# A transformer block with cross-attention and MLP on one core: batches 2 to 4 of the MLP loaded and normalised sooner, the steps between attention and MLP in another order

## The chip, the cores and the metric

The kernel runs on one core of a Trainium2 chip. The metric is device time in microseconds (us). A core has TensorE (PE: matmuls and transposes), VectorE (DVE), ScalarE (ACT), GpSimd (POOL) and SyncE (SP, which here issues the DMAs). Each engine works through its own queue in order, and waits by semaphores for results of the others and for transfers.

## The reference

One block of a diffusion transformer, with x and the context 16 x 256 x 256, a condition vector for each of 16 batches, 16 heads of 16 and an MLP of width 1024, all in fp32:

```python
c_proj = silu(c) @ W_mod + b_mod
shift_a, scale_a, gate_a, shift_m, scale_m, gate_m = split(c_proj, 6)
q, k, v = heads(modulate(_ln(x), shift_a, scale_a) @ W_qkv + b_qkv)
x = x + gate_a[:, None] * (softmax(q @ k.T * scale) @ v @ W_proj + b_proj)
q_c = heads(_ln(x) @ W_qc + b_qc)
k_c, v_c = heads(_ln(context) @ W_kvc + b_kvc)
x = x + (softmax(q_c @ k_c.T * scale) @ v_c @ W_cproj + b_cproj)
h = gelu(modulate(_ln(x), shift_m, scale_m) @ W_mlp1 + b_mlp1) @ W_mlp2 + b_mlp2
x = x + gate_m[:, None] * h
```

## The kernel before

**Units and beats.** The attention is cut into 32 units, one for each batch and kind: self-attention (names with `_s`, then the batch) and cross-attention (`_c`), the last units being c10 (unit 26) to c15 (unit 31). A unit is 8 beats. In a beat `beat(n, k)` TensorE computes scores of the next unit (`s`, to find the row maxima `mx`) and of this one (`st`), while pieces of the neighbours are laid between: the projections of unit n+2, the transposes of n+3, the layernorm of n+4, the load of n+5, the output projection of n-1. The table `PLAN` names these pieces by short words, beat by beat. fp32 products are made of a high and a low part (`xTh`, `xTl`; `wkch`, `wkcl`), so each is three matmuls; POOL makes most of the splits (a CAST for the high part, a subtraction for the low one).

**Order.** All instructions go through `InOrder` (line 51 in the profile), which keeps each engine's program order as written. So an instruction that waits holds up everything behind it on its engine. Only ScalarE is left to the compiler's scheduler from chunk 23 of the MLP on (`'AP': 23`).

**The MLP.** After unit 31 comes the tail: 16 batches of 4 chunks, numbered 0 to 63. With chunk i TensorE runs the first matmul (`ph_b_c`, 12 matmuls) of chunk i+2 and the second (`s` or `st` from `hh`, `hl`; 12 matmuls) of chunk i-1; ScalarE makes gelu twice (`hf` in fp32, `hh` rounded), POOL the rest `hl`. First matmuls of batches 0 and 1 run before that, in units 30 and 31 (`ps_h`, parked in `hk` and `v`); ph_1_3 is the last of them. Before a batch's first matmul its rows must be loaded back from DRAM (`mlp_load`, tile `x2_b`; the store is `x2d`), given the projection's bias (`mlp_bias`, POOL, x + cb), measured (`mlp_stats`, DVE, `st_m`, `mv_m`, with a reciprocal root `rs_m` on POOL) and normalised (`mlp_apply`, DVE, `xn_m`). Batch 2 is transposed by TensorE (`mlp_T(2)`). From batch 3 on `mlp_apply` transposes blocks on DVE (`blk_m`) and sends them by four DMAs to `turned`; `mlp_fetch` brings them back by four DMAs (`raw_m`), and `mlp_T` scales them on ScalarE (`xTf_m`) and splits them on POOL into `wkch`, `wkcl` (even batches) or `wqch`, `wqcl` (odd ones), which ph reads.

**Where batches 0 to 4 are prepared.** Batches 0 and 1 take the places of units 32 and 33 in the beats: load by the word `ld` at beat 1 and bias by `c2` at beat 2 of the unit four ahead of them. The steps of batch 2 hang on numbers in `E_['M']` = (7, 9, 13, 15), for load, bias, statistics and apply: number p means unit 31 + p // 16, beat (p % 16) // 2, here beats 3, 4, 6 and 7 of unit 31. Batch 3 is loaded after the last beat; its bias comes with chunk 0, its statistics with chunk 1, its `mlp_apply` with chunk 3, its fetch with chunk 4. Between the last beat and chunk 0 stand the last attention pieces: `av_part` (TensorE's `o`), `q.proj` (output projection of c14, `psP_c14`), then `o.turn(1)` and `o.norm(1)` (copy `oT_31_3`, transposes `psA1_c15`, normalised `A_c15`).

**The late query layernorm.** For the first and the last two cross units the layernorm of the query (`st_q`, `rs_q`, `xn_q`) is made one unit later than for the others, by ScalarE (words L1, L2, L3, with a factor `nb_q` on DVE); for the rest it is made on POOL (words e5, e6).

Of the kernel before, what the change touches and what calls it, by code (L numbers as in the profile page):

```python
# [21 lines left out]
def pixart_block(  # L22
# [8 lines left out]
    B, N, H = x.shape  # L31
# [76 lines left out]
    brow = const.tile([32, P], F32, name="brow")  # L108
# [147 lines left out]
    wm = []  # L256
# [9 lines left out]
    gm = []  # L266
# [850 lines left out]
    def beat(n, k):  # L1117
# [133 lines left out]
    for i, (b, c) in enumerate(chunks):  # L1251
        ACT.on = i < E_['AP']
        if 2 < i < len(chunks) - 1:
            mlp_gelu(*chunks[i + 1])
        if i in turns:
            mlp_T(turns[i])
        if c == 3 and b + 3 in BY_DVE:
            mlp_apply(b + 3)
        if c == 0 and b + 2 in BY_DVE:
            mlp_fetch(b + 2)  # L1260
        if i in firsts:
            mlp_first(*chunks[firsts[i]])
        if i > 0:
            mlp_second(*chunks[i - 1])
        for f in pst.get(i, ()):
            f()
        ahead = b + 2 if 2 < b + 2 < B else None
        soon = ahead if ahead and ahead in BY_DVE else None
        if c == 0 and ahead and not soon:
            mlp_bias(ahead)  # L1270
        if c == 0 and b + 3 in BY_DVE:
            mlp_bias(b + 3)
        if c == 1:
            if b + 1 < B:
                mlp_gates(b + 1)
            if b + 3 in BY_DVE:
                mlp_stats(b + 3)
                M[b + 3].ln.pow()
            if ahead and not soon:
                mlp_stats(ahead)  # L1280
        if c == 2 and ahead and not soon:
            M[ahead].ln.pow()
        if c == 2 and 4 <= b + 4 < B:
            mlp_load(b + 4)
        if c == 3:
            if ahead and not soon:
                mlp_apply(ahead)
            mlp_residual(b)
# [49 lines left out]
```

## Time and profile before

| | us |
|---|---|
| runs | 742.74, 743.11, 747.35 |
| median | 743.11 |
| the profiled execution | 747.66 |
| its span | 745.9 |
| outside the span | 1.76 |

The profile shows one execution, which is 4.55 us above the median of the runs. Times in a row are its start and its duration, counted from the start of the span; a name has its buffer number left out, so `xn_m` stands for every batch. A bracket behind a row is the idle time of the engine ahead of it and what ended that. All rows have line 51, since the helper records every operation.

### The profile page before, as it was taken

How to read it: one execution, taken by the hardware profiler on the slowest of the kernel's cores; microseconds unless marked ns; L12 is line 12 of the kernel's file. 1: busy time of each engine (PE TensorE's matmuls, PEld its weight loads, DVE VectorE, ACT ScalarE, POOL GpSimd, SP SyncE). 2: the span in 40 equal slices, each digit the busy share in tenths (PEclk: the TensorE clock that was granted, in tenths of full speed). 3: DMA queues.
4: the chain of work that ended last, by engine and by line, in shares of the span. 5: the costliest groups of instructions: out<-in, count | busy, mean ns of one | idle time of the engine just before them, and what ended most of it. 6: DMA issues, size and time to landing. Idle time of an engine off the chain costs nothing.

```text
span 745.9 us, 25386 instructions
## 1 busy us (share of the span) xinstructions
PE 731.3 (98%) x10092; PEld 644.4 (86%) x10092; DVE 569.1 (76%) x1165; ACT 563.6 (76%) x978; POOL 520.2 (70%) x636
## 2 busy tenths in 40 slices
PE   9999999999999999999999999999999998999997
PEld 8778888888888888888888888878879998999997
DVE  4888888988888888888889889898727664546542
ACT  4278888888888888888888888888895665666663
POOL 6756676857667485665758678667566887788872
PEclk9999999999999999999999999999999999999999
DMA  6755445443544545354544545544122544443430
GB/s 207 199 147 154 133 127 143 121 131 102 171 118 127 145 117 146 107 165 131 143 135 121 163 127 162 155 122 122 59 73 58 156 132 104 109 127 97 114 81 34
DMA packets 108906, 94.81 MB, mean 127 GB/s; under 512 B 36914, under 2 KB 92756, under 8 KB 108788
## 3 DMA queue, kind: packets, MB, share of 16 engines
q1 hardware_dynamic: 108308, 92.27, 44.5%
q8 instruction: 80, 1.31, 0.7%
q0 software_dynamic: 192, 0.52, 0.3%
q10 hardware_dynamic: 288, 0.39, 0.2%
q14 instruction: 38, 0.31, 0.1%
HBM read 30.38 MB, written 11.86 MB: 57 GB/s over the span
## 4 chain that ended last, share of the span: by engine, by line
PE 92%; DVE 2%; ACT 1%; POOL 1%; issue 1%; DMA 1%; SPq 1%; ACTq 0%; DVEq 0%; POOLq 0%
PE s L51 17%; PE st L51 16%; PE o L51 16%; PE ph L51 9%; PE ps_q L51 5%; PE ps_qc L51 4%; PE ps_kc L51 3%; PE ps_P_s L51 3%; PE ps_v_c L51 3%; PE ps_k L51 3%; PE ps_v_s L51 2%; PE ps_P_c L51 2%; PE ps_h L51 1%; PE psT_q L51 1%; PE psA_c L51 1%
## 5 line engine op out<-in xcount | busy, mean ns | idle before, releaser
L51 DVE TENSOR_REDUCE mx<-s 128x2 f32<-128x512 f32 x504 | 324.3, 682 | 63.3 <-PE s L51 56.8
L51 ACT ACTIVATE pt<-st 128x1024 f32<-128x1024 f32 x252 | 259.0, 1028 | 17.5 <-PE st L51 11.7
L51 PE MATMUL s<-big 63*128 63x256 f32 (+1 forms) x1024 | 184.1, 298 | 0.6 <-DVE mx L51 0.4
L51 PEld LDWEIGHTS s<-big 63*128 63x128 f32 (+1 forms) x1024 | 133.6, 185 | 19.8 <-DVE l_kc L51 6.6
L51 PE MATMUL st<-big 64*128 64x256 f32 (+1 forms) x1024 | 133.8, 298 | 0.3 <-ACT pt L51 0.2
L51 PE MATMUL o<-pt,v 128*32 128x256 f32 x2048 | 123.8, 382 | 0.0
L51 PEld LDWEIGHTS st<-big 64*128 64x128 f32 (+1 forms) x1024 | 95.5, 185 | 16.3 <-issue 12.9
L51 POOL TENSOR_TENSOR hl<-hf,hh 128x512 fp32r<-128x512 f32 x64 | 86.5, 1359 | 28.0 <-ACT hh L51 28.0
L51 PEld LDWEIGHTS o<-pt,v 128*32 128x32 f32 x2048 | 60.0, 109 | 41.5
L51 ACT ACTIVATE hh<-ph,bT 128x256 fp32r<-128x256 f32 x114 | 48.0, 474 | 24.3 <-PE st L51 12.4
L51 ACT ACTIVATE hf<-ph,bT 128x256 f32<-128x256 f32 x114 | 47.7, 472 | 22.5 <-PE ph L51 22.5
L51 ACT COPY oT<-o 128x512 f32<-128x512 f32 x63 | 36.9, 586 | 32.6 <-PE o L51 32.6
L51 PE MATMUL st<-big,hh 128*128 128x256 f32 x256 | 47.6, 285 | 0.0
L51 PE MATMUL ph<-wkch,wself 128*128 128x256 f32 x224 | 44.8, 284 | 2.4 <-ACT hh L51 2.4
L51 DVE TENSOR_SCALAR xn_m<-x,mv_m,rs_m 128x256 f32<-128x256 f32 x28 | 31.5, 1165 | 20.3 <-POOL rs_m L51 20.3
L51 PE MATMUL s<-big,hh 128*128 128x256 f32 x256 | 46.8, 282 | 0.0
L51 PE MATMUL ph<-wqch,wself 128*128 128x256 f32 x224 | 44.6, 282 | 1.3 <-ACT hh L51 1.3
L51 PE MATMUL ps_k<-xTh_s,wself 64*128 64x256 f32 (+1 forms) x232 | 43.9, 294 | 0.0
L51 PE MATMUL ps_q<-xTh_s,wself 64*128 64x256 f32 (+1 forms) x240 | 39.7, 283 | 0.4 <-DVE l_q L51 0.4
L51 PEld LDWEIGHTS st<-big,hh 128*128 128x128 f32 x256 | 39.9, 193 | 0.0
L51 POOL CAST xTh_c<-y_c 128x512 fp32r<-128x512 f32 x16 | 9.8, 612 | 43.1 <-ACT y_c L51 43.1
L51 PE MATMUL ps_v_s<-wself,xTh_s 64*128 64x256 f32 x224 | 39.2, 294 | 0.0
(249 smaller groups left out, 2500.1 us busy)
## 6 DMA issues: line engine op xcount, KB each, us to landing
big<-h_kc SPq DMA_DIRECT2D x64, 128.0 KB
big<-h_qc SPq DMA_DIRECT2D x64, 128.0 KB
big<-h_k SPq DMA_DIRECT2D x62, 128.0 KB
big<-h_q SPq DMA_DIRECT2D x62, 128.0 KB
big<-l_k SPq DMA_DIRECT2D x32, 128.0 KB
big<-l_q SPq DMA_DIRECT2D x32, 128.0 KB
g<-gd SPq DMA_DIRECT2D x16, 256.0 KB
c<-in_ctx_dram SPq DMA_DIRECT2D x16, 256.0 KB
```

The lines of the kernel that those rows point to most:

```text
L51: i = f(*a, **k)
```

## The change

In six places the order is written anew; the matmuls stay the same.

- The four steps of batch 2 (`E_['M']`) move from unit 31 to unit 30, beats 3 and 6 (load, bias), and to unit 31, beats 0 and 2 (statistics, apply).
- Batch 3 is loaded at beat 4 of unit 31, its bias made ahead of the first gelu, its statistics right after `o.norm(1)`, its `mlp_apply` with chunk 1, its fetch with chunk 2. Batch 4 is loaded after the last beat.
- `q.proj(0)` and `q.proj(1)` come ahead of `av_part(last, 2)` and `(last, 3)`, and `mlp_first` of chunk 7 (ph_1_3) behind them and the first gelu. So TensorE runs psP_c14, o, ph_1_3 instead of ph_1_3, o, psP_c14.
- c14 is no longer late: its query layernorm is made in unit 26 on POOL instead of in unit 27 on ScalarE.
- Batches 0 and 1 are loaded by the word `lc` at beat 5 of the unit before, and their bias is made at beat 1 (`c1`) instead of beat 2.
- Loads of batches 5 and up are issued ahead of the batch's gate load (`gm`) instead of behind it.

```diff
...
                 return tc.keep_in_program_order(i) if self.on else i
             return issue
 
-    E_ = {'M': (7, 9, 13, 15),
...
+    E_ = {'M': (-10, -4, 1, 5),
...
 
     PE = InOrder(nc.tensor, True)
     ACT, DVE, POOL, SP = (InOrder(e, True) for e in (nc.scalar, nc.vector, nc.gpsimd, nc.sync))
...
     def end(p, f, *a):
         at_end[p // 16 - 1, p % 16].append(lambda: f(*a))
 
+    end(8, mlp_load, 3)
     for p, f in zip(E_['M'], (mlp_load, mlp_bias, lambda b: mlp_stats(b, True), mlp_apply)):
         end(p, f, 2)
 
...
         lc = q4 if q4 and q4.kind == "c" else None
         ls = q4 if q4 and q4.kind in ("s", "m") and q4.ln else None
         lx = q3 if q3 and q3.kind == "c" else None
-        late = lx and lx.b in (0, B - 2, B - 1)
-        early = lc if lc and lc.b not in (0, B - 2, B - 1) else None
-        c5 = unit(n + 5)
+        late = lx and lx.b in (0, B - 1)
+        early = lc if lc and lc.b not in (0, B - 1) else None
+        c5 = later_unit(n + 5)
         ln = lambda v, i: lambda *a: v.ln[i].steps
 
         def attention(v, hf):
...
             "pe": on(p2, lambda: p2.end()), "hadd": on(p2 and (p2.n == nu - 3), lambda: (p2.add(), p2.store())),
             "add": on(p3, lambda: p3.add()), "gate": on(p1, lambda: p1.gate()),
             "store": on(p3, lambda: p3.store()), "begin": lambda: cur.post.begin(),
-            "ld": on(ls and n > 0, lambda: load(ls)),
-            "lc": on(c5 and c5.kind == "c", lambda: load(c5)),
-            "c1": on(lc, lambda: lc.ln[0].steps[0]()),
-            "c2": on(lc or ls and ls.kind == "m", lambda: [f() for f in lc.ln[0].steps[1:]] if lc else mlp_bias(ls.b)),
+            "ld": on(ls and n > 0 and ls.kind == "s", lambda: load(ls)),
+            "lc": on(c5 and c5.kind != "s" and (c5.kind == "c" or c5.ln), lambda: load(c5)),
+            "c1": on(lc or ls and ls.kind == "m", lambda: lc.ln[0].steps[0]() if lc else mlp_bias(ls.b)),
+            "c2": on(lc, lambda: [f() for f in lc.ln[0].steps[1:]]),
             "s1": on(ls, lambda: ls.ln[0].steps[0]()),
             "s6": on(ls, lambda: ls.ln[0].steps[1]()),
             "s7": on(ls, lambda: ls.ln[0].steps[2]()),
...
     M[0].h[3] = tail[2].K.ps.rearrange("p (j n) -> p j n", j=2)
     for b in range(2):
         M[b].xT = M[b].src.xT
-    mlp_load(3)
+    mlp_load(4)
     mlp_gates(0)
     first_at = 7
-    mlp_first(*chunks[first_at])
+    q.proj(0)
+    q.proj(1)
     av_part(last, 2)
     av_part(last, 3)
+    mlp_bias(3)
     mlp_gelu(*chunks[0])
-    q.proj(0)
-    q.proj(1)
+    mlp_first(*chunks[first_at])
     mlp_gelu(*chunks[1])
     mlp_gelu(*chunks[2])
     mlp_gelu(*chunks[3])
     q.finish()
     o.turn(1)
     o.norm(1)
-    pst = {1: (lambda: mlp_T(2), o.aT.turn, o.aT.high, o.aT.low_dve), 4: (lambda: o.proj(0), lambda: o.proj(1), o.finish)}
+    mlp_stats(3)
+    M[3].ln.pow()
+    pst = {1: (lambda: mlp_T(2), o.aT.turn, o.aT.high, o.aT.low_dve, lambda: mlp_apply(3)),
+           2: (lambda: mlp_fetch(3),), 4: (lambda: o.proj(0), lambda: o.proj(1), o.finish)}
     turns = {}
     turns.update((NCH * b, b + 1) for b in range(2, B - 1))
     firsts = {5: 8}
...
             mlp_gelu(*chunks[i + 1])
         if i in turns:
             mlp_T(turns[i])
-        if c == 3 and b + 3 in BY_DVE:
+        if c == 3 and b > 0 and b + 3 in BY_DVE:
             mlp_apply(b + 3)
-        if c == 0 and b + 2 in BY_DVE:
+        if c == 0 and b > 1 and b + 2 in BY_DVE:
             mlp_fetch(b + 2)
         if i in firsts:
             mlp_first(*chunks[firsts[i]])
...
         soon = ahead if ahead and ahead in BY_DVE else None
         if c == 0 and ahead and not soon:
             mlp_bias(ahead)
-        if c == 0 and b + 3 in BY_DVE:
+        if c == 0 and b > 0 and b + 3 in BY_DVE:
             mlp_bias(b + 3)
         if c == 1:
             if b + 1 < B:
                 mlp_gates(b + 1)
-            if b + 3 in BY_DVE:
+            if b > 0 and b + 3 in BY_DVE:
                 mlp_stats(b + 3)
                 M[b + 3].ln.pow()
             if ahead and not soon:
                 mlp_stats(ahead)
         if c == 2 and ahead and not soon:
             M[ahead].ln.pow()
-        if c == 2 and 4 <= b + 4 < B:
+        if c == 0 and 4 < b + 4 < B:
             mlp_load(b + 4)
         if c == 3:
             if ahead and not soon:
```

VectorE at the end of unit 31, from the second half of c14's normalisation (`rc1`, `A_c14`) to the projection's gate (`t1_c14`), before:

```order
L51 RECIPROCAL rc1_c14_12183<-psA1_c14_12135 128x16
L51 TENSOR_TENSOR A_c14_12053<-psA1_c14_12135,rc1_c14_12183 128x4x64
L51 BN_STATS st_m2_12285<-x2_2_12186 128x6 x2
L51 BN_AGGR mv_m2_12288<-st_m2_12285 128x2 x2
L51 RECIPROCAL rc0_c15_12315<-psA0_c15_12260 128x16
L51 TENSOR_TENSOR A_c15_12314<-psA0_c15_12260,rc0_c15_12315 128x4x64
L51 TENSOR_SCALAR xn_m2_12318<-x2_2_12186,mv_m2_12288,rs_m2_12291 128x256 x2
L51 COPY oT_31_3_12355<-o_31_2_12338 128x512
L51 TENSOR_TENSOR t1_c14_12396<-psP_c14_12363,xg_14_9475 128x512
```

After, from the statistics of batch 2:

```order
L51 BN_STATS st_m2_12098<-x2_2_11894 128x6 x2
L51 BN_AGGR mv_m2_12101<-st_m2_12098 128x2 x2
L51 TENSOR_SCALAR xn_m2_12172<-x2_2_11894,mv_m2_12101,rs_m2_12104 128x256 x2
L51 RECIPROCAL rc1_c14_12198<-psA1_c14_12147 128x16
L51 TENSOR_TENSOR A_c14_12056<-psA1_c14_12147,rc1_c14_12198 128x4x64
L51 RECIPROCAL rc0_c15_12320<-psA0_c15_12274 128x16
L51 TENSOR_TENSOR A_c15_12319<-psA0_c15_12274,rc0_c15_12320 128x4x64
L51 COPY oT_31_3_12357<-o_31_2_12340 128x512
L51 TENSOR_TENSOR t1_c14_12399<-psP_c14_12327,xg_14_9475 128x512
```

The statistics and `xn_m2` moved from between c14 and the copy `oT_31_3` to ahead of c14's second half; the copy follows `A_c15` directly.

VectorE from there on to `xn_m3`, before:

```order
L51 TENSOR_TENSOR A_c15_12314<-psA1_c15_12399,rc1_c15_12404 128x4x64
L51 TENSOR_SCALAR xTf_m2_12425<-psT_m2_12420,sc1_103,cpT_101 128x256 x2
L51 TENSOR_TENSOR wkcl_96<-xTf_m2_12425,wkch_95 128x512
L51 TENSOR_TENSOR xTl_ac15_12437<-psT_ac15_12431,xTh_ac15_12436 128x512
L51 BN_STATS st_m3_12442<-x2_3_12321 128x6 x2
L51 BN_AGGR mv_m3_12445<-st_m3_12442 128x2 x2
L51 TENSOR_SCALAR xn_m3_12471<-x2_3_12321,mv_m3_12445,rs_m3_12448 128x8x32 x2
```

After:

```order
L51 TENSOR_TENSOR A_c15_12319<-psA1_c15_12402,rc1_c15_12407 128x4x64
L51 BN_STATS st_m3_12410<-x2_3_12229 128x6 x2
L51 BN_AGGR mv_m3_12413<-st_m3_12410 128x2 x2
L51 TENSOR_SCALAR xTf_m2_12436<-psT_m2_12431,sc1_103,cpT_101 128x256 x2
L51 TENSOR_TENSOR wkcl_96<-xTf_m2_12436,wkch_95 128x512
L51 TENSOR_TENSOR xTl_ac15_12448<-psT_ac15_12442,xTh_ac15_12447 128x512
L51 TENSOR_SCALAR xn_m3_12451<-x2_3_12229,mv_m3_12413,rs_m3_12416 128x8x32 x2
```

The statistics of batch 3 (`st_m3`, `mv_m3`) moved from behind `xTl_ac15` to ahead of `xTf_m2`.

POOL between the bias of batch 2 and that of batch 3, the last ahead of the MLP's `hl`, before (`big2` holds the second weight, `y_ac14` is c14's transposed output):

```order
L51 TENSOR_TENSOR x2_2_12186<-x2_2_12186,cb_106 128x512
L51 CAST xTh_ac14_12250<-y_ac14_12248 128x512
L51 TENSOR_TENSOR xTl_ac14_12251<-y_ac14_12248,xTh_ac14_12250 128x512
L51 TENSOR_TENSOR big2_77<-w2_7_11676,big2_77 128x512
L51 TENSOR_SCALAR rs_m2_12291<-mv_m2_12288 128x2
L51 TENSOR_TENSOR rs_m2_12291<-rs_m2_12291,mhalf_73 128x2
L51 TENSOR_TENSOR hl_0_0_12359<-hf_0_0_12357,hh_0_0_12358 128x512
L51 TENSOR_TENSOR hl_0_1_12378<-hf_0_1_12376,hh_0_1_12377 128x512
L51 TENSOR_TENSOR hl_0_2_12384<-hf_0_2_12382,hh_0_2_12383 128x512
L51 TENSOR_TENSOR hl_0_3_12390<-hf_0_3_12388,hh_0_3_12389 128x512
L51 TENSOR_TENSOR x2_3_12321<-x2_3_12321,cb_106 128x512
```

After, from `rs_m2` on, batch 2's bias being further ahead, behind c13's split:

```order
L51 TENSOR_SCALAR rs_m2_12104<-mv_m2_12101 128x2
L51 TENSOR_TENSOR rs_m2_12104<-rs_m2_12104,mhalf_73 128x2
L51 TENSOR_TENSOR big2_77<-w2_4_11725,big2_77 128x512
L51 TENSOR_TENSOR t1_c13_12145<-t1_c13_12145,xg_13_8712 128x512
L51 TENSOR_TENSOR big2_77<-w2_5_11154,big2_77 128x512
L51 CAST xTh_ac14_12264<-y_ac14_12262 128x512
L51 TENSOR_TENSOR xTl_ac14_12265<-y_ac14_12262,xTh_ac14_12264 128x512
L51 TENSOR_TENSOR big2_77<-w2_7_11676,big2_77 128x512
L51 TENSOR_TENSOR x2_3_12229<-x2_3_12229,cb_106 128x512
L51 TENSOR_TENSOR hl_0_0_12362<-hf_0_0_12360,hh_0_0_12361 128x512
```

The bias of batch 2 and `rs_m2` moved ahead of the last weight splits and c14's split; the bias of batch 3 moved from behind `hl_0_3` to ahead of `hl_0_0`.

More of the change, by code (lines that the diff above doesn't have):

```diff
@@ L53, in __getattr__ @@
             return issue
-    E_ = {'M': (7, 9, 13, 15), 'CUT': 8, 'LN': {'s': 'pool', 'c': 'pool', 'q': 'pool'}, 'ON': (1, 1, 1), 'L0': -16, 'L1': 1, 'S0': -7, 'A0': 0, 'T0': 1, 'S1': 5, 'A1': 7, 'L2': 9, 'T1': 9, 'S2': 32, 'AP': 23, 'DV': (0, 1), 'HP': (1, 0), 'BZ': {}, 'AV': {1: [(1, 2), (1, 3)], 9: [(0, 0), (0, 1)]}, 'AHEAD': (0, 0, 0, 0, 0, 2), 'TW': {(21, 6): 'cb', (23, 6): 'u1', (25, 1): 'u0', (25, 7): 'u2', (27, 1): 'u3', (27, 4): 'h2p', (27, 5): 'h3p', (28, 0): 'l2d', (28, 3): 'u5 h1p', (28, 4): 'h0p', (29, 0): 'l3', (29, 1): 'l0', (29, 3): 'l1d', (29, 6): 'u7', (29, 7): 'u4 u6 h4p', (30, 1): 'h5p h6d', (30, 7): 'l6', (31, 0): 'h7p', (31, 1): 'l4', (31, 2): 'l5', (31, 6): 'l7'}, 'XP': 1, 'IL': 1, 'MF': 0, 'SH': 4, 'RAMP': 1, 'HA': 1, 'MP': 16, 'W': (7, 1, 0, 0), 'PRE': 'z0qp z0kp load rest ld2 one0 silu b12 brow L0a turn L0b b4 L0d scale T0t sc1 hik lok L1a T0h L1b T0l b4 shift hiq K0a L1d bk loq K0m K0h K0x0 K0x1 K0y0p K0y1p T1t K0l T1h K0l0 K0l1 bq T1l Q0a Q0m Q0h Q0x0 Q0y0p Q0x1 Q0y1p Q0l Q0l0 Q0l1 z1kp z1qp K1a K1b hiv lov Q1a Q1b K1x0 K1x1 K1y0 K1y1 K1l K1l0 K1l1 Q1x0 Q1x1 Q1y0 Q1y1 Q1l Q1l0 Q1l1 L2a L2b L2c V0a V0b bv b9 ld3', 'SL': {(-1, 0): 'V1a', (-1, 1): 'T2t T2h T2p vone z2kp z2qp', (-1, 2): 'V1b', (-1, 3): 'rest wm', (-1, 4): 'M0 rest one1 ld4', (-1, 5): 'K2a L3a', (-1, 6): 'K2m L3b L3p L3c', (-1, 7): 'mods sc2 one2 rest', (0, 0): 'gm rest', (0, 1): 'rest', (0, 4): 'rest', (0, 6): 'rest', (1, 0): 'rest', (1, 5): 'rest'}}
@@ new lines, in pixart_block @@
+    E_ = {'M': (-10, -4, 1, 5), 'CUT': 8, 'LN': {'s': 'pool', 'c': 'pool', 'q': 'pool'}, 'ON': (1, 1, 1), 'L0': -16, 'L1': 1, 'S0': -7, 'A0': 0, 'T0': 1, 'S1': 5, 'A1': 7, 'L2': 9, 'T1': 9, 'S2': 32, 'AP': 23, 'DV': (0, 1), 'HP': (1, 0), 'BZ': {}, 'AV': {1: [(1, 2), (1, 3)], 9: [(0, 0), (0, 1)]}, 'AHEAD': (0, 0, 0, 0, 0, 2), 'TW': {(21, 6): 'cb', (23, 6): 'u1', (25, 1): 'u0', (25, 7): 'u2', (27, 1): 'u3', (27, 4): 'h2p', (27, 5): 'h3p', (28, 0): 'l2d', (28, 3): 'u5 h1p', (28, 4): 'h0p', (29, 0): 'l3', (29, 1): 'l0', (29, 3): 'l1d', (29, 6): 'u7', (29, 7): 'u4 u6 h4p', (30, 1): 'h5p h6d', (30, 7): 'l6', (31, 0): 'h7p', (31, 1): 'l4', (31, 2): 'l5', (31, 6): 'l7'}, 'XP': 1, 'IL': 1, 'MF': 0, 'SH': 4, 'RAMP': 1, 'HA': 1, 'MP': 16, 'W': (7, 1, 0, 0), 'PRE': 'z0qp z0kp load rest ld2 one0 silu b12 brow L0a turn L0b b4 L0d scale T0t sc1 hik lok L1a T0h L1b T0l b4 shift hiq K0a L1d bk loq K0m K0h K0x0 K0x1 K0y0p K0y1p T1t K0l T1h K0l0 K0l1 bq T1l Q0a Q0m Q0h Q0x0 Q0y0p Q0x1 Q0y1p Q0l Q0l0 Q0l1 z1kp z1qp K1a K1b hiv lov Q1a Q1b K1x0 K1x1 K1y0 K1y1 K1l K1l0 K1l1 Q1x0 Q1x1 Q1y0 Q1y1 Q1l Q1l0 Q1l1 L2a L2b L2c V0a V0b bv b9 ld3', 'SL': {(-1, 0): 'V1a', (-1, 1): 'T2t T2h T2p vone z2kp z2qp', (-1, 2): 'V1b', (-1, 3): 'rest wm', (-1, 4): 'M0 rest one1 ld4', (-1, 5): 'K2a L3a', (-1, 6): 'K2m L3b L3p L3c', (-1, 7): 'mods sc2 one2 rest', (0, 0): 'gm rest', (0, 1): 'rest', (0, 4): 'rest', (0, 6): 'rest', (1, 0): 'rest', (1, 5): 'rest'}}
```

## The prediction

> **What bounds the kernel now.** I read the page first, then busy time by stretch, then TensorE's timeline for its gaps, the chain that ended last, and the other engines' timelines at each gap. The page:
>
> ```profile
> PE 731.3 (98%) x10092; PEld 644.4 (86%) x10092; DVE 569.1 (76%) x1165; ACT 563.6 (76%) x978; POOL 520.2 (70%) x636
> ```
>
> TensorE is busy for 731.3 of 745.9 us. The change issues the same matmuls, so only the 14.6 us of gaps, and the clock, can move. By stretch (PE busy first, granted clock after POOL):
>
> ```profile
> core 0: us, PE busy (x) PEld busy (x) DVE busy (x) ACT busy (x) POOL busy (x), PEclk, DMA share, GB/s
> 100.00:490.00 390.00, 389.85 (x6403) 331.28 (x6404) 340.61 (x735) 330.46 (x512) 271.89 (x372) 1.00 0.48 135
> 490.00:580.00 90.00, 86.89 (x1194) 74.64 (x1187) 63.59 (x120) 69.00 (x118) 60.11 (x66) 1.00 0.32 90
> 580.00:620.00 40.00, 38.72 (x326) 38.35 (x325) 26.06 (x42) 26.76 (x64) 35.56 (x32) 1.00 0.51 136
> 620.00:660.00 40.00, 37.65 (x306) 37.44 (x305) 19.88 (x34) 22.79 (x55) 31.29 (x30) 0.96 0.41 109
> ```
>
> From 100 to 490 us the gaps come to 0.15 us: nothing is to be won there, only lost. The change works between 465 and 590 us. TensorE's own rows, the gap and its releaser in brackets, show what there is to win:
>
> ```profile
> 501.93 0.27 PE L51 MATMUL psm<-ident,mx 64*128 64x64 f32 x1 [0.84 <-ACT oT L51]
> 560.15 0.66 PE L51 MATMUL psA_c<-ident,oT 128*128 128x128 f32 x4 [1.06 <-DVE oT L51]
> 578.11 0.39 PE L51 MATMUL st<-big,hl 128*128 128x256 f32 x1 [0.56 <-POOL hl L51]
> 583.22 0.35 PE L51 MATMUL ph<-wqch,wself 128*128 128x256 f32 x1 [0.83 <-ACT hh L51]
> 584.03 0.38 PE L51 MATMUL ph<-wqcl,wself 128*128 128x256 f32 x1 [0.45 <-POOL wqcl L51]
> 626.20 0.38 PE L51 MATMUL ph<-wkch,wself 128*128 128x256 f32 x1 [2.35 <-ACT hh L51]
> ```
>
> The first five, 0.84 + 1.06 + 0.56 + 0.83 + 0.45 = 3.74 us, lie where the change works and are the most that it can win in its own place. The sixth is far behind it, and is dearer than its 2.35 us. The chain of waits in order of time, there (start, duration, what):
>
> ```profile
> 621.01 1.42 PE ph L51 x12
> 626.20 1.77 PE ph L51 x12
> 627.96 2.57 PE st L51 x12
> 630.53 1.72 PE ph L51 x12
> ```
>
> Twelve such matmuls take 1.42 us, and after the gap 1.77, 2.57 and 1.72: 0.35 + 1.15 + 0.30 = 1.80 us more. The whole event costs 2.35 + 1.80 = 4.15 us. Its cause is a late transfer, here with batch 3's for comparison (SP's issue of the fetch, then ScalarE's first use):
>
> ```profile
> 577.22 1.72 SPq L51 DMA_DIRECT2D raw_m<-turned  x4
> 580.53 1.09 ACT L51 ACTIVATE xTf_m<-raw_m,cpT,sc 128x256 f32<-128x256 f32 x2 [3.81 <-DMA raw_m<-turned]
> 617.60 1.93 SPq L51 DMA_DIRECT2D raw_m<-turned  x4
> 623.60 1.09 ACT L51 ACTIVATE xTf_m<-raw_m,cpT,sc 128x256 f32<-128x256 f32 x2 [4.61 <-DMA raw_m<-turned]
> ```
>
> Batch 3's fetch was used 580.53 − 578.94 = 1.6 us after its last issue, batch 7's 623.60 − 619.53 = 4.1 us after. The profiled execution took 747.66 us, the median is 743.11, one of the three runs shows 747.35: the 4.55 us between profile and median is about this event (4.15), so I take it to be present in two of the four executions seen and absent from the median. That is an inference: no row shows a run without it.
>
> **Part 1, batch 2 a unit sooner, and o and projection ahead of the last first matmul.** The 1.06 us at 560.15:
>
> ```profile
> 551.22 1.29 POOL L51 TENSOR_TENSOR x<-x,cb 128x512 f32<-128x512 f32 x1 [3.38 <-DMA x<-x2d]
> 553.14 1.31 POOL L51 TENSOR_TENSOR xTl_ac<-y_ac,xTh_ac 128x512 fp32r<-128x512 f32 x1
> 550.79 0.61 ACT L51 COPY y_ac<-psT_ac 128x512 f32<-128x512 f32 x1
> 555.53 1.93 PE L51 MATMUL o<-pt,v 128*32 128x256 f32 x32
> 556.84 2.66 DVE L51 TENSOR_SCALAR xn_m<-x,mv_m,rs_m 128x256 f32<-128x256 f32 x2 [2.73 <-POOL rs_m L51]
> 559.42 0.68 DVE L51 COPY oT<-o 128x512 f32<-128x512 f32 x1
> ```
>
> TensorE's o ends near 557.4, but VectorE copies it (oT) only at 559.42, behind xn_m2, which waited for POOL's bias, which waited for batch 2's load. Now xn_m2 runs in unit 31, and the copy can start at 557.5. The reordering also puts the first matmul ph_1_3 (1.42 us) between o and the transposes that need oT: 1.5 us of cover for a copy of 0.68. The gap goes: **−1.06 us**. What is late next: the projection (psP) now comes first, at 553.9, and needs POOL's split of y_ac. That copy ends at 551.40, and POOL, no longer held by the load, can finish the cast (0.6) and xTl_ac (1.31) by 553.4, ahead of it.
>
> The moved steps are not free. POOL's bias (1.29) lands at about 538.4, behind c13's split, which TensorE needs first, with POOL's next wait (for ScalarE's t_c, until 545.3) to absorb it. xn_m2 goes ahead of A_c14:
>
> ```profile
> 546.24 0.42 DVE L51 TENSOR_TENSOR A_c<-psA_c,rc_c 128x256 f32<-128x256 f32 x1
> 549.55 0.21 PE L51 MATMUL psT_ac<-ident,A_c 64*128 64x64 f32 x1
> ```
>
> A_c ends at 546.66 and is used at 549.55: 2.9 us of slack against xn_m2's 2.66 us, which can begin at about 543.8 (rs_m2 ready) and so pushes A_c by about 0.5 us. Price 0; if all 2.66 us came late, still 0.
>
> **Part 2, batch 3 sooner.** Its chain, link by link, and hl's wait:
>
> ```profile
> 567.11 0.22 POOL L51 TENSOR_SCALAR rs_m<-mv_m 128x2 f32<-128x2 f32 x1 [4.00 <-DVE mv_m L51]
> 568.15 2.68 DVE L51 TENSOR_SCALAR xn_m<-x,mv_m,rs_m 128x256 f32<-128x256 f32 x2 [1.14 <-POOL rs_m L51]
> 571.60 2.65 SPq L51 DMA_DIRECT2D turned<-blk_m  x4
> 575.81 0.22 POOL L51 TENSOR_SCALAR rs_m<-mv_m 128x2 f32<-128x2 f32 x1 [2.11 <-DVE mv_m L51]
> 581.69 0.61 POOL L51 CAST wqch<-xTf_m 128x512 fp32r<-128x512 f32 x1 [1.03 <-ACT xTf_m L51]
> 582.38 1.59 POOL L51 TENSOR_TENSOR wqcl<-xTf_m,wqch 128x512 fp32r<-128x512 f32 x1
> ```
>
> The statistics now stand on VectorE right behind A_c15 instead of behind xTl_ac15, so rs_m3 is ready by about 562.8, behind the four hl of batch 0, instead of 568.1. xn_m3 then waits only for VectorE's own order: it follows xTl_ac15, at about 565.1 instead of 568.15, 3.05 us sooner. Transpose, `turned` and fetch follow at the same distance: landing 577.5 instead of 580.53, wqcl ready at 583.97 − 3.05 = 580.9. TensorE came to ph at 583.22 − 0.83 = 582.39; without the two gaps before (1.06 + 0.56) it comes at 580.8. Left over: 0 to 0.3 us, so of 0.83 + 0.45 = 1.28 us I win **−1.1**. The 0.56 us at 578.11 goes too: hl_1_3 stands behind rs_m4, which waited 2.11 us for mv_m4, itself behind xn_m3; 3.05 us sooner is more than 2.11. **−0.56**. The one instruction that stands in a worse place is POOL's bias of batch 3 (1.29), now ahead of hl_0_0 instead of behind hl_0_3; it fits between the last weight split and gelu's first output (556.5), price 0, unless its load is late (rival C). On SP the gate load gm_1 (0.4 us of issue) moves behind `turned`, ahead of the fetch, which waits some 3 us there: 0.
>
> **Part 3, biases of batches 0 and 1 a beat sooner.** The 0.84 us at 501.93:
>
> ```profile
> 498.98 1.28 POOL L51 TENSOR_TENSOR x<-x,cb 128x512 f32<-128x512 f32 x1
> 499.13 1.15 DVE L51 SCALAR_TENSOR_TENSOR nb_q<-mv_q,rs_q 128x2 f32<-128x2 f32 x1
> 500.20 1.18 POOL L51 CAST wself<-w 128x512 fp32r<-128x512 f32 x2
> 500.32 1.09 ACT L51 ACTIVATE xn_q<-xg,nb_q,rs_q 128x256 f32<-128x256 f32 x2 [1.01 <-DVE nb_q L51]
> ```
>
> nb_q has two elements a lane, yet takes 1.15 us: it ends at 500.28, when POOL's bias ends (500.26). ScalarE's xn_q and oT wait behind it. With the bias a beat sooner the two casts (0.59 each) stand there. At best the whole 0.84 goes, at worst nothing (nb_q waits for both); nearest is one cast, so about **−0.5**. Batch 1's bias moves with it, where TensorE shows no gap: 0. On SP the two loads move ahead of one send of maxima and one batch of keys each, and batch 2's ahead of two sends of maxima and two stores; a load's issue is 0.42 us (its row stands under rival C), and SP waits there for the next send's data anyway: 0. The rule on this is in the Trainium skill, SBUF — State Buffer, section Who interferes with whom: a VectorE instruction with two SBUF inputs and a GpSimd one that reads SBUF exclude each other for a whole instruction. By that rule the 1.15 us is one wait for the bias, the trace agrees, and the sum here is a wait of one cast, the 0.5 taken above. The same rule speaks against part 1, since xn_m2 and POOL's weight splits would take turns in unit 31; by it A_c comes 1.3 us later still, 1.8 in all, under its 2.9.
>
> **Part 4, c14's query layernorm from unit 27 (ScalarE) to unit 26 (POOL).** POOL gains a subtraction factor and two normalisations, as in
>
> ```profile
> 523.80 1.09 POOL L51 TENSOR_SCALAR xn_m<-x,less_m,rs_m 128x256 f32<-128x256 f32 x2
> ```
>
> about 1.3 us with the small one, and its rs pair (0.94) comes sooner; ScalarE loses 1.09. All of c1 to c13 already go this way between 100 and 490 us, with 0.15 us of gaps. So 0; bounds −0.2 to +2.3 (all of POOL's added work in the open).
>
> **Part 5, loads of batches 5 and up ahead of the gate load.** One issue of 0.45 us swaps with another, everything else in the tail keeps its order: 0, and batch 7's late fetch is as possible as before.
>
> **Sum.** 1.06 + 0.56 + 1.1 + 0.5 = 3.2 us. Against the profiled execution's own time: 747.66 − 3.2 = 744.5 with the event at 626, 740.3 without. Against the median: 743.11 − 3.2 = 739.9. The median is what is forecast: **739.9 us**.
>
> **Rivals.** A: the late fetch falls into the changed kernel's median. For it: by the inference above it was there in two of four executions, and the tail is left as it is. Against: it was absent from the median, and by the first windows row of the tail, 580 to 620, the same kind of fetch ran with 1.28 us of gaps in all, both batch 3's. 739.9 + 4.15 = 744.1. The Trainium skill, TensorE: Matmul & The Clock Gate, section HAM oscillation, gives idle gaps over some 3.4 us as what halves the clock. By that rule a gap of 2.35 us would cost 2.35 and A would end at 742.3; the trace disagrees here, with 1.80 us of slower matmuls behind a gap of 2.35.
>
> B: the change does less than it says, because other work is late at the same places: only part 1 comes through, 743.11 − 1.06 = 742.1. For it: batch 3's raw landing and wqcl are within 0.3 us of TensorE by my walk.
>
> C, slower: POOL's bias of batch 3 holds hl_0_0. The nearest row for its load:
>
> ```profile
> 547.02 0.42 SPq L51 DMA_DIRECT2D x<-x2d  x1
> ```
>
> issued at 547.02, used at 551.22: 4.2 us. Batch 3's goes out near 547.5 and is wanted at 554.6; POOL has 1.5 us to spare before second(0) near 559.5. From a landing later than 556.1, 8.6 us after issue, TensorE waits; it decides above 3.2 us of wait, or 2.35 with the 1.80 us of halved clock, so from a landing at 558.5: 743.11 − 3.2 + 2.35 + 1.80 = 744.1, and a landing at 561 gives 746.6. Against: twice the row's time is needed.
>
> **Chances.** The forecast (738.8 to 741.2, from 501.93 fully or not won and 0 to 0.3 at 583) 0.61; A 0.2; B (741.2 to 743.1) 0.11; C 0.05 (744 to 747); more than 3.74 us won, below 738.6, 0.03. The range 738.6 to 744.6 holds the first, B and most of A. One per cent, about what a measurement of this kernel can tell from no change, is 7.4 us: below 735.7 nothing here leads, 0.02; above 750.5 only A and C with a second gap, 0.03; within, 0.95.
>
> **What would show it.** TensorE's row of psA_c without a gap; A_c14 used without a wait; rs_m3 near 562.8 and xn_m3 near 565; no gap at hl_1_3 and under 0.3 us at ph of batch 3; nb_q under 0.7 us beside a cast. Wrong it would be by a new gap at psT_ac (xn_m2), at s<-big,hl of batch 0 (the bias), at ps_qc of c13 (part 4), or a median with the late fetch.

## The result: 5.4 us won where 3.2 were forecast

The changed kernel takes 738.38 us (median of 6, 737.74 to 739.28), the kernel before 743.75 (median of 6, 742.74 to 747.35): a ratio of 0.9921, with a 95% interval of 0.9907 to 0.9936. That is 5.4 us, within the 1% that was forecast, but 1.5 us below the forecast of 739.9 and 0.2 us below the range.

The page and the busy time by stretch of the changed kernel (its profiled execution took 737.81 us, its span is 736.0), to be held against the rows of before:

```profile
PE 727.4 (99%) x10092; PEld 641.9 (87%) x10092; DVE 567.6 (77%) x1164; ACT 562.6 (76%) x976; POOL 521.6 (71%) x639
```

```profile
490.00:580.00 90.00, 89.22 (x1224) 77.68 (x1217) 64.27 (x126) 73.17 (x129) 65.73 (x70) 1.00 0.37 102
580.00:620.00 40.00, 40.00 (x342) 40.00 (x341) 25.25 (x41) 26.82 (x65) 33.98 (x32) 1.00 0.48 128
620.00:660.00 40.00, 40.00 (x341) 40.00 (x340) 23.48 (x40) 25.76 (x63) 35.07 (x33) 1.00 0.43 115
```

From 580 to 660 us TensorE has no idle time left (80.00 of 80 us busy; in the kernel before 76.37), and from 490 to 580 us its idle time falls from 3.11 to 0.78 us. Of its timeline after 460 us, these are all rows of after with a gap in brackets; the rest of the 0.78 lies in pieces that have none, the smallest bracket seen being 0.15 us:

```profile
494.23 0.50 PE L51 MATMUL s<-big 63*128 63x256 f32 x3 [0.22 <-DVE mx L51]
537.48 0.36 PE L51 MATMUL ps_P_c<-wcph,xTh_ac 64*128 64x256 f32 x1 [0.20 <-POOL xTl_ac L51]
```

All five gaps that the prediction counted are out of the brackets, and so is the sixth, at 626, that it left where it was. Of the first, 0.14 us is left: the last matmul ahead of psm ends at 501.31 as drawn, and psm starts at 501.45. The places where steps moved, in the changed kernel's timelines:

```profile
499.35 0.45 DVE L51 SCALAR_TENSOR_TENSOR nb_q<-mv_q,rs_q 128x2 f32<-128x2 f32 x1
542.82 1.70 DVE L51 TENSOR_SCALAR xn_m<-x,mv_m,rs_m 128x256 f32<-128x256 f32 x2 [2.60 <-POOL rs_m L51]
545.26 0.42 DVE L51 TENSOR_TENSOR A_c<-psA_c,rc_c 128x256 f32<-128x256 f32 x1
556.62 0.69 DVE L51 COPY oT<-o 128x512 f32<-128x512 f32 x1 [4.80 <-ACT hh L51]
563.79 1.80 DVE L51 TENSOR_SCALAR xn_m<-x,mv_m,rs_m 128x256 f32<-128x256 f32 x2
574.86 1.09 ACT L51 ACTIVATE xTf_m<-raw_m,cpT,sc 128x256 f32<-128x256 f32 x2 [0.41 <-DMA raw_m<-turned]
576.92 1.30 POOL L51 TENSOR_TENSOR wqcl<-xTf_m,wqch 128x512 fp32r<-128x512 f32 x1
```

nb_q takes 0.45 us beside the cast, where it took 1.15 beside the bias; xn_m2 ends at 544.5, before its neighbour A_c14 has its input; the copy oT no longer stands behind other work of VectorE, which was idle for 4.80 us ahead of it; batch 3 is fetched 5.7 us sooner than before (574.86 instead of 580.53).

**Where the 5 us come from.** The same matmul can be found in both traces, and the difference of its start is the distance that the changed kernel has won up to there. Starts of TensorE's rows (the last two of the chain, the others of the timeline), with a second trace of the kernel before (the run `e0_before`, below):

| TensorE's row | before | before, 2nd | after | won so far (first trace) | step |
|---|---|---|---|---|---|
| o, ahead of nb_q's place | 498.12 | 498.17 | 498.34 | -0.22 | |
| o, in the next unit | 515.68 | 515.71 | 515.18 | 0.50 | 0.72 |
| o, in unit 30 | 540.72 | 540.73 | 539.75 | 0.97 | 0.47 |
| psA_c of c15 | 560.15 | 560.05 | 557.93 | 2.22 | 1.25 |
| ph behind hl_1_3's place | 579.55 | | 576.47 | 3.08 | 0.86 |
| s behind ph of batch 3 | 585.59 | 585.35 | 580.72 | 4.87 | 1.79 |

The sum of the steps is 5.09 us (4.80 by the second trace of before, and 5.15 by the second trace of the changed kernel, `a_again`), where the prediction had counted 3.2 and held 3.74 for the most that there was. The -0.22 in the first row is not the change's doing: ahead of the places that it touches, TensorE's rows differ by up to 1.3 us between the traces of all runs (the first o behind 456 us starts at 456.83 to 458.13).

### The profile page after: what moved, and what is told of

The parts are those of the page before. It is cut to its first block, busy times and chain, and to the rows that moved or that the text cites. A ratio compares the mean times of both kernels' runs of the same rounds, so it can differ in the third digit from the quotient of the medians.

```text
span 736.0 us, 25389 instructions
## 1 busy us (share of the span) xinstructions
PE 727.4 (99%) x10092; PEld 641.9 (87%) x10092; DVE 567.6 (77%) x1164; ACT 562.6 (76%) x976; POOL 521.6 (71%) x639
## 4 chain that ended last, share of the span: by engine, by line
PE 94%; DVE 2%; issue 1%; ACT 1%; DMA 1%; POOL 1%; SPq 0%; POOLq 0%; ACTq 0%; DVEq 0%
PE s L51 17%; PE st L51 16%; PE o L51 16%; PE ph L51 11%; PE ps_qc L51 4%; PE ps_q L51 4%; PE ps_kc L51 3%; PE ps_P_s L51 3%; PE ps_k L51 3%; PE ps_v_c L51 3%; PE ps_v_s L51 3%; PE ps_P_c L51 2%; PE ps_h L51 1%; PE psT_q L51 1%; PE psA_s L51 1%
## 5 line engine op out<-in xcount | busy, mean ns | idle before, releaser
L51 DVE TENSOR_SCALAR xn_m<-x,mv_m,rs_m 128x256 f32<-128x256 f32 x28 | 28.8, 1067 | 19.0 <-POOL rs_m L51 19.0
L51 POOL CAST xTh_ac<-y_ac 128x512 fp32r<-128x512 f32 x15 | 9.2, 612 | 46.6 <-ACT y_ac L51 46.6
```

Of the source, the lines that this page charges most:

```text
L51: i = f(*a, **k)
```

## The experiments

Times are medians. The changed kernel has two sets of executions, with medians of 738.38 and 737.83; over all 11 the median is 738.1, and what an undone part brings back is counted from there. "By distance" means the difference in start of the same matmul in two traces, as in the table.

**The kernel before, again.** Edit: none.

> The kernel before itself, unchanged, for a second trace of it. Theory: its gaps between 500 and 590 us (0.84, 1.06, 0.56, 0.83, 0.45 in the first trace) come again in every execution, within 0.1 us, and the 2.35 us gap at 626 only where a fetch lands late; without it the span is about 741.7. Rival: the gap at 626 is part of every execution, and the runs differ for another reason.

Measured: 744.32 us (742.93 to 745.07, 10 executions; ratio 0.9996, 0.9984 to 1.0008). The profiled one, 744.75, is 0.4 us above the median, the second highest of the ten. Its rows on TensorE and ScalarE:

```profile
560.05 0.65 PE L51 MATMUL psA_c<-ident,oT 128*128 128x128 f32 x4 [0.96 <-DVE oT L51]
582.95 0.35 PE L51 MATMUL ph<-wqch,wself 128*128 128x256 f32 x1 [0.65 <-ACT hh L51]
625.35 0.38 PE L51 MATMUL ph<-wkch,wself 128*128 128x256 f32 x1 [1.75 <-ACT hh L51]
```

```profile
622.75 1.09 ACT L51 ACTIVATE xTf_m<-raw_m,cpT,sc 128x256 f32<-128x256 f32 x2 [4.00 <-DMA raw_m<-turned]
```

The gaps come again at the same places, 0.1 to 0.2 us smaller at two of them. The gap behind batch 7's fetch is there too, 1.75 us long. Its whole cost, by distance to the changed kernel, is 2.03 us; without it the execution would have taken 742.7, less than any of the ten. So most of them probably hold something of it, though only this one has a trace. The gap as such doesn't separate the first profiled execution from the median: what that had more was a longer wait and the halved clock.

**Part 3 undone** (loads and biases of batches 0 and 1).

```diff
-        c5 = later_unit(n + 5)
+        c5 = unit(n + 5)
...
-            "ld": on(ls and n > 0 and ls.kind == "s", lambda: load(ls)),
-            "lc": on(c5 and c5.kind != "s" and (c5.kind == "c" or c5.ln), lambda: load(c5)),
-            "c1": on(lc or ls and ls.kind == "m", lambda: lc.ln[0].steps[0]() if lc else mlp_bias(ls.b)),
-            "c2": on(lc, lambda: [f() for f in lc.ln[0].steps[1:]]),
+            "ld": on(ls and n > 0, lambda: load(ls)),
+            "lc": on(c5 and c5.kind == "c", lambda: load(c5)),
+            "c1": on(lc, lambda: lc.ln[0].steps[0]()),
+            "c2": on(lc or ls and ls.kind == "m", lambda: [f() for f in lc.ln[0].steps[1:]] if lc else mlp_bias(ls.b)),
```

> The changed kernel with part 3 undone: loads and biases of batches 0 and 1 where they were. Theory, from the distance between the two traces: 0.74 us come back at nb_q and 0.56 us around 518 us, where a weight split on VectorE (1.64 us instead of 0.69) stands beside batch 1's bias; together +1.3 us, 739.7. Rival as on record: only the bracketed gap counts, +0.5 to 0.84, and batch 1's bias costs nothing. Second rival: 0, the gap had gone by chance.

Measured: 739.26 us (738.92 to 740.58), +1.2; by distance 0.68 us come back at nb_q and 0.47 around 518. The bracketed gap is back at its old size, and so is the second place, which has no bracket:

```profile
501.99 0.27 PE L51 MATMUL psm<-ident,mx 64*128 64x64 f32 x1 [0.84 <-ACT oT L51]
515.07 1.29 POOL L51 TENSOR_TENSOR xTl_m<-y_m,xTh_m 128x512 fp32r<-128x512 f32 x1
515.27 1.64 DVE L51 TENSOR_TENSOR wself<-w,wself 128x512 fp32r<-128x512 f32 x1
517.92 0.75 PE L51 MATMUL s<-big 63*128 63x256 f32 x4
```

In the changed kernel the same three instructions read:

```profile
514.75 0.69 DVE L51 TENSOR_TENSOR wself<-w,wself 128x512 fp32r<-128x512 f32 x1
514.97 1.62 POOL L51 TENSOR_TENSOR xTl_m<-y_m,xTh_m 128x512 fp32r<-128x512 f32 x1
517.38 0.40 PE L51 MATMUL s<-big 63*128 63x256 f32 x4
```

Whichever of VectorE's weight split and POOL's `xTl_m` comes first takes its own time (VectorE 0.69, POOL 1.29); the other ends nearly its own time after it (VectorE 0.55 us after POOL, POOL 1.15 after VectorE). The Trainium skill, SBUF — State Buffer, section Who interferes with whom, says just that of two such instructions, and that the order of issue decides who waits; the trace agrees. Where POOL is first, VectorE's row maxima (mx) start at 516.83 instead of 515.36, and the four matmuls `s`, which the profile shows waiting for mx, take 0.75 us instead of 0.40: the wait lies inside the row of a busy TensorE. So the theory holds, and the rival on record (0 for batch 1's bias) falls.

**The order of projection, o and first matmul undone.**

```diff
-    q.proj(0)
-    q.proj(1)
+    mlp_first(*chunks[first_at])
     av_part(last, 2)
     av_part(last, 3)
     mlp_bias(3)
     mlp_gelu(*chunks[0])
-    mlp_first(*chunks[first_at])
+    q.proj(0)
+    q.proj(1)
```

> The changed kernel with the first matmul ph_1_3 ahead of o, and the projection psP behind it, as before. Theory: 0 (within 0.3 us), since the copy oT no longer stands behind xn_m2 and the projection covers it as well as ph_1_3 does. Rival: the order itself was what covered the copy, +1.0 us or more.

Measured: 738.24 us (737.5 to 738.69): nothing comes back, and its trace has no gap at psA_c. The new order on TensorE, which the prediction counted as cover, earns nothing by itself; with xn_m2 out of the way psP covers the copy as ph_1_3 does.

**Batch 2 put back into unit 31.**

```diff
-    E_ = {'M': (-10, -4, 1, 5),
...
+    E_ = {'M': (7, 9, 13, 15),
...
```

> The changed kernel with the four steps of batch 2 back in unit 31. Theory: oT waits behind xn_m2 again and TensorE with it, 1.06 to 1.31 us come back, or more, since batch 3's bias now stands behind batch 2's on POOL. Rival: with ph_1_3 between o and the transposes the wait is covered, 0.

Measured: 740.77 us, and in two groups: 739.36, 739.38, 739.96 and 741.57, 741.59, 741.72. The profiled execution (741.59) is of the upper group; VectorE and TensorE, then ScalarE:

```profile
558.51 0.68 DVE L51 COPY oT<-o 128x512 f32<-128x512 f32 x1
559.25 0.66 PE L51 MATMUL psA_c<-ident,oT 128*128 128x128 f32 x4 [1.33 <-DVE oT L51]
622.24 0.39 PE L51 MATMUL ph<-wkch,wself 128*128 128x256 f32 x1 [1.91 <-ACT hh L51]
```

```profile
619.64 1.09 ACT L51 ACTIVATE xTf_m<-raw_m,cpT,sc 128x256 f32<-128x256 f32 x2 [4.16 <-DMA raw_m<-turned]
```

The copy is late again and TensorE with it, although ph_1_3 now stands between: the rival falls. By distance this costs 1.36 us, which is the lower group's +1.3; the profiled execution has the gap behind batch 7's fetch on top, 1.91 us long and dearer by distance (2.18). For the other two of the upper group that is an inference from their times.

**Batch 3 put back** (its load, bias, statistics, apply and fetch, and batch 4's load; in the parts not shown the conditions `b > 0` and `b > 1` of the loop go).

```diff
-    end(8, mlp_load, 3)
-    mlp_load(4)
+    mlp_load(3)
-    mlp_bias(3)
...
-    mlp_stats(3)
-    M[3].ln.pow()
-    pst = {1: (lambda: mlp_T(2), o.aT.turn, o.aT.high, o.aT.low_dve, lambda: mlp_apply(3)),
-           2: (lambda: mlp_fetch(3),), 4: (lambda: o.proj(0), lambda: o.proj(1), o.finish)}
+    pst = {1: (lambda: mlp_T(2), o.aT.turn, o.aT.high, o.aT.low_dve), 4: (lambda: o.proj(0), lambda: o.proj(1), o.finish)}
...
-        if c == 0 and 4 < b + 4 < B:
+        if c == 0 and 4 < b + 4 < B or c == 2 and b == 0:
```

> The changed kernel with batch 3's load, bias, statistics, apply and fetch (and batch 4's load) where they were. Theory, from the distance between the two traces: 0.8 us come back at hl_1_3 and 1.8 us at ph of batch 3, +2.6 us, though their bracketed gaps come to 0.56 and 1.28 only. Rival as on record: the brackets, +1.84 at most.

Measured: 740.68 us (739.74 to 745.63; three of 12 executions at 742.26 and above), +2.6. The brackets of its trace come to only 0.88:

```profile
576.17 0.39 PE L51 MATMUL st<-big,hl 128*128 128x256 f32 x1 [0.59 <-POOL hl L51]
580.77 0.36 PE L51 MATMUL ph<-wqch,wself 128*128 128x256 f32 x1 [0.29 <-ACT hh L51]
```

The rival, +1.84 at most, falls by the median, but the theory's sizes hold only in half. By distance the trace (740.54) gives back 0.86 us at hl_1_3, as expected, and 0.95 at ph of batch 3 instead of 1.8. The rest of this trace's distance lies elsewhere: 0.3 us ahead of the changed places and 0.54 in the tail, in waits without a bracket. Measured against TensorE, batch 3's fetch is used 0.5 us sooner in this run than in the kernel before, and wqcl takes 1.28 us instead of 1.59. So about 0.8 us of the step at ph comes from other parts of the change than batch 3's own steps; from which is not shown.

**c14's query layernorm put back to ScalarE.**

```diff
-        late = lx and lx.b in (0, B - 1)
-        early = lc if lc and lc.b not in (0, B - 1) else None
+        late = lx and lx.b in (0, B - 2, B - 1)
+        early = lc if lc and lc.b not in (0, B - 2, B - 1) else None
```

> The changed kernel with c14's query layernorm back in unit 27 on ScalarE. Theory: 0 (within 0.3 us), there was no gap in either trace. Rival: it made POOL or ScalarE free where something else waited, 0.3 us or more come back, seen as distance to the changed kernel's trace from about 475 us on.

Measured: 738.18 us (737.76 to 739.15): 0, as forecast for part 4.

**The gate load ahead of the batch loads again.**

```diff
-        if c == 0 and 4 < b + 4 < B:
+        if c == 2 and 4 < b + 4 < B:
```

> The changed kernel with the loads of batches 5 and up behind the gate load again. Theory: 0, and runs as close together as the changed kernel's (737.7 to 739.3). Rival: the gate load ahead of them is what makes a fetch land late, so the spread of the kernel before comes back, with runs at 741 or more and a gap like that at 626 us in some.

Measured: 739.28 us, 11 executions from 737.95 to 743.23, four of them above 740.5. The changed kernel has none above 739.3 in 11. The theory (0 and as close together) falls as to the spread. Of the four executions above 740.5 none has a trace, and the profiled one, 739.28, has no late fetch: it was 1.0 us behind the changed kernel before 460 us already (o at 458.13 instead of 457.13), and the clock of the opening shows the likely reason. Busy time from 30 to 50 us, in this run and then in the changed kernel (granted clock third from the end):

```profile
30.00:50.00 20.00, 19.69 (x193) 14.33 (x192) 16.18 (x32) 8.99 (x15) 12.16 (x15) 0.91 0.55 158
```

```profile
30.00:50.00 20.00, 19.48 (x210) 14.74 (x211) 17.39 (x35) 9.67 (x17) 12.11 (x15) 1.00 0.56 162
```

So 1.0 of the 1.5 us between these two profiled executions is no price of the gate load, whose place lies far behind the opening; what the other executions had is not shown.

**ScalarE in program order to the end,** in the changed kernel, in the kernel before, and together with the gate load put back.

```diff
... (one entry of the table E_)
-'AP': 23,
+'AP': 64,
...
```

> The changed kernel with ScalarE kept in program order to the end. Theory: the scheduler's order from chunk 23 on puts the scaling of a fetched batch ahead of gelus, so that ScalarE waits for the fetch (11.3 us in ten waits in the changed kernel's trace); in program order these waits shrink below 3 us. The time stays the same within 0.5 us where no fetch is late. Rival: the scheduler's order saves waits of TensorE that the program order brings back, +1 us or more.

> The kernel before with ScalarE kept in program order to the end and nothing else changed. Theory: TensorE's gap near 626 us is what ScalarE's wait for batch 7's fetch leaves after 2.25 us of cover (waits of 4.61, 4.00 and 4.16 us gave gaps of 2.35, 1.75 and 1.91), and it is part of the median of the kernel before; in program order there is no such wait, the median falls by 1.8 to 2.2 us to about 742.2, and the runs lie within 1.5 us. Rival: the median holds no such gap, it stays at 743.5 to 744.3.

> The changed kernel with the gate load ahead of the batch loads again and ScalarE in program order to the end. Theory: the executions at 740.6 to 743.2 that the gate load's place alone gave come from late fetches, and in program order nobody waits for them: all executions within 736.5 to 738.7. Rival: the spread has another cause and stays.

Measured: the changed kernel 737.64 us (736.51 to 738.52), the gate load put back 737.77 (737.63 to 738.75), the kernel before 742.89, beside 744.7 without the edit. Batch 7's scaling on ScalarE, in the changed kernel and then in program order:

```profile
616.03 1.09 ACT L51 ACTIVATE xTf_m<-raw_m,cpT,sc 128x256 f32<-128x256 f32 x2 [1.91 <-DMA raw_m<-turned]
```

```profile
619.50 1.09 ACT L51 ACTIVATE xTf_m<-raw_m,cpT,sc 128x256 f32<-128x256 f32 x2
```

The scheduler had placed it two chunks of gelu (four instructions) early, so ScalarE waits for the fetch with gelus behind it; over the whole kernel these waits fall from 11.3 us in ten to 0.6 in one, as expected. Wait and TensorE's gap go together: 4.61 and 2.35, 4.16 and 1.91, 4.00 and 1.75, and no gap there in the traces with a wait of 2.23 or less. About 2.25 us are covered. In program order the wait is gone, and with the gate load put back none of five executions is above 738.75. That speaks for the late fetch as the cause of the executions above 740.5, but doesn't show it: where four of 11 were so long, five without one come by chance about once in ten times. In the changed kernel itself program order wins little (0.4 us, within the spread): nothing is late there. For the kernel before it is worth more, but not as cleanly as expected: 7 of 12 executions lie at 742.3 to 743.0, below the lowest of the 23 beside them (743.23), the others at 744.1 to 749.2, and the interval of the ratio (0.9975 to 1.001) holds 1. The trace of one of those others (744.08) has no gap in the tail beyond 590 us. It was 0.9 us behind the first trace of before by 458 us already, and another gap had grown, from 1.06 us:

```profile
561.81 0.66 PE L51 MATMUL psA_c<-ident,oT 128*128 128x128 f32 x4 [1.78 <-DVE oT L51]
```

There batch 2's load was used 4.93 us after its issue instead of 4.20, and everything up to the copy oT came later by that. So in the kernel before more than one wait hangs on when a transfer lands.

**The new load order alone, in the kernel before.**

```diff
-        if c == 2 and 4 <= b + 4 < B:
+        if c == 2 and b == 0 or c == 0 and 4 < b + 4 < B:
```

> The kernel before with the loads of batches 5 and up ahead of the gate load and nothing else changed. Theory: this order is what brings batch 7's fetch in time, the median falls by 1.8 to 2.2 us to about 742.2 and the trace shows no gap near 626 us. Rival: it has no part in it, the median stays at about 744 and the gap with it; then the time at which the fetch goes out decides.

Measured: 743.95 us beside 744.7 (ratio 0.999, 0.9976 to 1.0004). Its trace (743.55) has no gap near 626, batch 7's fetch was in time; but the median moved by 0.75 us and not by 2, within its interval. Neither theory nor rival is settled by this.

**The changed kernel again.** Edit: none.

> The changed kernel again, for more executions beside those of the other kernels. Theory: batch 7's fetch lands within 1.9 us of its last issue, so no execution is above 740. Rival: late fetches are only rarer in it, and one or two of the executions lie at 740 to 743.

Measured: 737.83 us (737.73 to 738.82, 5 executions; ratio 0.9914, 0.9901 to 0.9926). None above 740, as expected.

## Why the prediction was right and wrong

The mechanisms of the main parts held: xn_m2 behind the late load held the copy oT; batch 3's chain was what made ph and hl wait; a bias beside nb_q made VectorE wait; c14's move costs nothing; none of the new waits came true, neither xn_m2 ahead of A_c14, nor batch 3's bias ahead of hl_0_0, nor POOL's added work in unit 26. The sizes were off, at three steps.

**The step that failed first:** "0.84 + 1.06 + 0.56 + 0.83 + 0.45 = 3.74 us, lie where the change works and are the most that it can win in its own place." A bracket is shorter than what the gap costs. In a row of matmuls without a wait the next one starts 0.12 us after the last, while each is drawn 0.28 us long. Three rows show it, psP_c of before, and ph and psA_c of after; the row of psA_c of before stands in the prediction:

```profile
558.45 0.64 PE L51 MATMUL psP_c<-wcph,xTl_ac 128*128 128x256 f32 x4
```

```profile
557.81 0.28 PE L51 MATMUL ph<-xTh_m,wself 128*128 128x256 f32 x1
557.93 0.60 PE L51 MATMUL psA_c<-ident,oT 128*128 128x128 f32 x4
```

After: the successor starts 0.12 us behind. Before: the last psP_c started at 558.45 + 0.36 = 558.81, so psA_c was due at 558.93 and came at 560.15: 1.22 us late, where the bracket says 1.06, since it counts from the drawn end. And the first matmul behind a gap is drawn longer (0.35 us at 583.22, 0.39 at 578.11, against 0.28), and its successor starts 0.22 to 0.23 us after it instead of 0.12. Together that is about 0.27 us a gap, an estimate from these rows; it also fits the gap behind batch 7's fetch, 1.75 us that cost 2.03 and 1.91 that cost 2.18. The distances agree: hl_1_3's 0.56 cost 0.86, the two gaps at ph 1.28 + 2 x 0.27 = 1.82 against 1.79 measured, psA_c's 1.06 cost 1.25. At 501.93 the gap didn't go, it shrank from 0.84 to 0.14 us, and 0.72 was won. There the prediction's 0.5 was small by its own rows: a cast of 0.59 in place of a bias of 1.28 lets nb_q end 0.69 sooner. The stated range had in fact gone beyond the step: 743.11 - 3.74 is 739.4, yet the forecast reached down to 738.8, and 738.6 stood for more than 3.74 won.

**The second:** "Batch 1's bias moves with it, where TensorE shows no gap: 0." It was 0.47 us. The waiting was there, in VectorE's 1.64 us for an operation of 0.69, and in a row of four matmuls that took 0.75 us.

With these, part by part: part 3, forecast 0.5, measured 0.72 + 0.47; part 1, 1.06 and 1.25; part 2, 1.66 and 0.86 + 1.79 (of which the run with batch 3 put back gives 0.86 + 0.95 back). The sum, 5.09, taken from the median that the prediction started from: 743.11 - 5.09 = 738.0, against 738.38 measured. So the size of the terms accounts for the miss. That it fits so closely is in part luck: 743.11 was the median of three executions, and other medians of the kernel before are 743.75, 744.32 and 744.7. From those the distance to the changed kernel is up to 6.6 us, and what goes beyond 5.1 is by the traces at least in part the tail, where the gap behind batch 7's fetch cost 2.03 us in one trace and 4.16 in the other.

**The third, in the rival A:** "I take it to be present in two of the four executions seen and absent from the median." The second trace has the gap, at 744.75 us. What separates 747.66 from the median is the longer wait and the clock. In the changed kernel the gap was absent from both traces and its executions are close together. Whether the change brought that about is not shown: with the old gate order four of 11 executions lie above 740.5, but none of them has a trace; with the new order alone in the kernel before the gain isn't clear; and with batch 2 put back the fetch was late in spite of the new order, and with batch 3 put back three of 12 executions were long too (742.26 to 745.63). What makes the fetch of batch 7 land 3.1 to 4.1 us after its last issue in three traces, and 1.7 to 1.9 in the others that show it, stays open.

Of rival B it can be said that it was wrong in its reason: batch 3's data came 5.7 us sooner and not 3, because xn_m3 took 1.80 us instead of 2.68 and began at 563.79 instead of the 565 of the walk, so nothing was left over at ph. TensorE came there at 579.13, sooner than the 580.8 of the walk, but wqcl was ready at 578.22 instead of 580.9 and was first used at 579.25.

## What to carry to other kernels

The idle time in TensorE's brackets was a lower bound of what each stall cost here; measure a stall by the start of the same instruction in two traces, or by the pitch of its neighbours with the restart added (together some 0.27 us above the bracket here). Where an engine reads as busy all the time, look for instructions that take longer than their equals, on it and on the engines that feed it: that is where the hidden waits are. A difference between one profile and a median isn't evidence on a single event; a second trace of the kernel before would have told it. And an undone part whose median comes back as expected can still come back in other places: look where, by distance.

## What the runs showed of the hardware

**The clock.** Two long gaps of TensorE in the tail left the clock alone, one didn't. Busy time by stretch around the gap of 1.75 us of the second trace of before, and then 2 us behind the gap of 2.35 of the first:

```profile
624.00:626.00 2.00, 0.65 (x5) 0.65 (x6) 0.00 (x0) 2.00 (x7) 0.63 (x1) 1.00 0.57 126
626.00:628.00 2.00, 2.00 (x19) 2.00 (x18) 0.00 (x0) 1.60 (x5) 1.84 (x2) 1.00 0.33 58
```

```profile
628.00:630.00 2.00, 2.00 (x11) 2.00 (x11) 0.00 (x0) 0.84 (x2) 1.92 (x3) 0.50 0.27 90
```

The granted clock stayed at 1.00 in the one and fell to 0.50 in the other (and stayed at 1.00 behind the 1.91 us with batch 2 put back). So in these three traces only the longest gap, by 0.44 us, was followed by slower matmuls, 1.8 us on top. Three events don't show that the length decides, and a gap in brackets isn't needed. In the run with the gate load put back the clock read 0.61 from 36 to 40 us, with TensorE busy all the time; the same four matmuls took 1.86 us there and 1.02 in the changed kernel (0.91 from 30 to 50 us, as here, stands in two more traces, `b2_gates` and `u6_order_kept`):

```profile
36.00:40.00 4.00, 4.00 (x19) 1.71 (x18) 2.30 (x7) 0.71 (x2) 3.27 (x6) 0.61 0.09 32
36.01 1.86 PE L51 MATMUL ps_cb<-wcp_f,bT 128*1 128x256 f32 x4
```

```profile
35.86 1.02 PE L51 MATMUL ps_cb<-wcp_f,bT 128*1 128x256 f32 x4
```

The Trainium skill, TensorE: Matmul & The Clock Gate, section HAM oscillation, sets the limit at some 3.4 us of idle time. Here the clock fell behind 2.35 us once, and in three traces without a gap in brackets, and the measurement decides.

**One port, two engines.** nb_q, of two elements a lane, took 1.15 us behind a POOL instruction of 1.28 and 0.45 behind one of 0.59, and a weight split 1.64 instead of 0.69. In each case VectorE's instruction ended after POOL's (nb_q by 0.02 us, the split by 0.55), and the cost reached TensorE by way of ScalarE or of the row maxima.
